# Moving the dense pieces among the steps of layer 1's attention

## The chip, the cores and the metric

The kernel runs on one core of one Trainium2 chip. Its time is the device time in microseconds; lower is better. Before the change three runs took 3043.94, 3046.15 and 3050.73 us, with a median of 3046.15 us.

## The reference

Two transformer layers run over `x` of 8 batches x 1024 tokens x 256. Layer 0 is windowed attention and a mixture of eight experts with a shared one. Layer 1, which the change touches, is block-sparse attention with 16 heads of 16 and blocks of 64 tokens, then a linear layer with ternary weights. Both layers normalize first and add their result to `x`.

```python
x = x + _L1_attn_ref(_layernorm(x, axis=-1), Wq, bq, Wk, bk, Wv, bv)
x = x + _L1_ffn_ref(_layernorm(x, axis=-1), weight, alpha, bias)
# in the attention: block 0 and block 15 of queries see all keys; block 1 and block 14
# see four blocks of keys; a block in the middle sees three neighbours, block 0 and block 15
```

The softmax subtracts each row's maximum, so scores are needed once for the maxima and again for the weights.

## The kernel before

**Two passes of scores.** `attention` (L377) serves both layers. A *round* of scores (`scores`, L392, matmuls at L404) makes the scores of one tile of 128 queries against the keys it meets, for four heads, in four PSUM tiles; VectorE takes the negated maximum of each (`maximum`, L414: L427, or L431 and L435 for the tile that sees all 1024 keys in two rounds). `into_q` (L439) transposes four tiles of maxima on TensorE (L442) and writes them into the queries (L446). Then `weights` (L448) makes the scores the other way round, with the maxima already subtracted (L459), in four PSUM tiles; ScalarE takes the exponential (L466), and GpSimd sets blocks that aren't met to zero (L1354). Two steps later `sums` (L477) multiplies them by v (L489), and `turned` (L501) transposes the result of half a batch (L504), which VectorE divides by the sum (L596, L597) and GpSimd adds to `x` (L1366).

**Steps.** One trip of the loop at L569 is a *step*. In layer 1 a batch has 4 groups of heads with 7 packs of weights and 9 rounds of scores, so 28 steps and 36 rounds: in every 7 steps, two have two rounds. In a batch these are steps 2, 6, 9, 13, 16, 20, 23 and 27. A step issues, in this order: weights (L459), the products of the step two back (L489), a round of scores (L404), what is due (transpositions L442 or L504), and, where there is a second round, the pieces due by the step's middle (`fill_until(step + 0.5)`) and that round; then the pieces due by its end (`fill_until(step + 1)`).

```python
                if some:
                    scores(*some.pop(0))
                for due, f in [x for x in later if x[0] <= step]:
                    later.remove((due, f))
                    f()
                if some:
                    fill_until(step + 0.5)
                    scores(*some.pop(0))
                fill_until(step + 1)
                step += 1
```

**Pieces.** What else a layer has to do is cut into pieces with due times in steps of the batch, written out by hand in `layer1` (L1400 to L1460). The order of issue is fixed by these times: all is recorded under a manual schedule, and each engine runs its instructions in that order. The pieces that use TensorE ("dense" ones: all 128 rows and columns) are, by line:

- L282, queries and keys (`qk_pieces`): 8 pieces for the second half of heads of batch b, in its own steps, and 8 for the first half of the next batch; ScalarE copies each out (L302, L314).
- L338, values (`v_pieces`): 8 pieces for the next batch; VectorE copies each out (L342).
- L235, transpositions of normalized rows (`norm_pieces`): piece `step(jp)` transposes pair jp-1, which ScalarE copies out (L248), and then has VectorE normalize pair jp (two instructions L223, one for each tile of the pair, into a buffer `xn` of which there are two).
- L1324, the ternary linear layer of the batch before (`product`): 8 pieces; VectorE adds each to `x` (L1330). Before it GpSimd adds the bias (L1319, `biased`).

Others use VectorE and GpSimd: statistics (L206 to L211), gathers of the experts' rows (an indirect DMA on GpSimd's queue, L1283) and their addition (L1291).

**PSUM.** Seven buffers of 128x512 (`ps_t`, L76) serve every tile but that of the products with v, in turn: a tile is written when the tile seven before it has been read.

Of the kernel before, what the change touches and what calls it, by code (L numbers as in the profile page):

```python
# [50 lines left out]
def seq_kernel(  # L51
# [135 lines left out]
    def piece(weight, f, *args, first=(), then=None):  # L187
        return weight, lambda: f(*args), first, then
# [1040 lines left out]
    def layer1():  # L1229
# [47 lines left out]
        def gathers(b):  # L1277

            w, ys = routed[b][2], {}

            def gather(j, n):
                y = ys[j, n] = pool.tile([128, D], F32, tag="y", name="y", bufs=16)
                nc.gpsimd.indirect_dma_start(  # L1283
                    out=y, out_offset=None, in_=made[:, :],
                    in_offset=bass.IndirectOffsetOnAxis(ap=place[b][:, n, j : j + 1], axis=0),
                )

            def add(j):
                xj = x_of[b][:, j, :]
                for n in range(2):  # L1290
                    nc.vector.scalar_tensor_tensor(  # L1291
                        xj, ys.pop((j, n)), w[:, j, n : n + 1], xj, ALU.mult, ALU.add
                    )

            return [
                piece(0.2, gather, j, n, first=[("placed", b)])
                for j in range(NT) for n in range(2)
            ], [piece(1.1, add, j, then=("added", b, j)) for j in range(NT)]

        def before_it(b):  # L1300
            qk_of[b], xnT_of[b] = {}, []
            norm = norm_pieces(
                b, "xnT2", xnT_of[b], "xnT", key_order=True,
                first=lambda jp: [("added", b, 2 * jp + 1)],
            )
            first = qk_pieces(b, 0, 1, wq_sb, wk_sb, xnT_of[b], qk_of[b])
            return gathers(b), norm, first, v_pieces(b, 1, wv_sb, xnT_of[b])
# [4 lines left out]
        def after_it(b):  # L1312

            xnT = []
            dst = out[b].rearrange("(t p) d -> p t d", p=128)

            def biased(jp):
                xp = x_of[b][:, pairs[jp], :]
                nc.gpsimd.tensor_tensor(xp, xp, bt, ALU.add)  # L1319

            def product(j):
                ps = psum_t()[:, 0:D]
                for kc in range(2):
                    nc.tensor.matmul(  # L1324
                        ps, lhsT=xnT[0][:, kc, j * 128 : (j + 1) * 128], rhs=wt_sb[:, kc, :],
                        start=(kc == 0), stop=(kc == 1),
                    )
                t = tile_at[j]
                xj = x_of[b][:, t, :]
                nc.vector.tensor_tensor(xj, ps, xj, ALU.add)  # L1330
                if j >= NT - 2:
                    nc.sync.dma_start(dst[:, t : t + 1, :], x_of[b][:, t : t + 1, :])
                elif j % 2:
                    nc.sync.dma_start(dst[:, t - 1 : t + 1, :], x_of[b][:, t - 1 : t + 1, :])

            norm = norm_pieces(
                b, "xnT", xnT, "normed", first=lambda jp: [("attended", b, 3, jp // 2)],
                tiles=tile_at, apart=b == B - 1,
            )
            return norm, [  # L1340
                piece(1.0, biased, jp, first=[("normed", b, jp)], then=("biased", b, jp))
                for jp in range(4)
            ], [piece(0.9, product, j, first=[("biased", b, j // 2)]) for j in range(NT)]
# [54 lines left out]
        def combining(gathered, x, at, adds, b):  # L1398

            gather, add = gathered  # L1400
            return [(0, [x], [piece(0.0, load, b)]), (0, at, gather), (0, adds, add)]

        beside = []
        for b in range(B + 1):
            lists = []
            if b == 0:
                (gather, add), (stats, scaled), first, values = before_it(0)

                rest = [piece(x[0], x[1]) for x in left_over]

                def some(n):
                    return [rest.pop(0) for _ in range(n)]

                begun = gather[:]
                for j, n in enumerate((3, 2, 1, 2, 1, 2, 1, 1)):
                    begun += some(n) + add[j : j + 1] + (stats[j // 2 : j // 2 + 1] if j % 2 else [])
                for x in scaled:
                    begun += [x] + (some(1) if len(rest) > 1 else [])
                lists.append((-1, -1e-6, begun + first + rest))
                lists.append((-0.95, -0.1, values))  # L1420
            if b < B:
                lists.append((
                    0, [0.4, 1.4, 2.2, 3.3, 4.4, 5.4, 6.2, 7.6],
                    qk_pieces(b, 1, 1, wq_sb, wk_sb, xnT_of[b], qk_of[b]),
                ))
            if b == B:
                (stats, scaled), biases, products = after_it(b - 1)
                scaled, turned = scaled[:4], scaled[4:]
                lists.append((
                    0, [-1.9, -0.9, -0.8, -0.7, 0.9, 0.92, 0.94, 0.96, 1.8, 1.9] + [2.5] * 14,  # L1430
                    stats[:2] + scaled[:2] + turned[:1] + biases[:1] + turned[1:2] + biases[1:2]
                    + products[:4] + stats[2:] + scaled[2:] + turned[2:] + biases[2:] + products[4:],
                ))
            elif b > 0:
                (stats, scaled), biases, products = after_it(b - 1)
                lists.append((0, [1.6, 2.8, 4.6, 5.5], stats))
                lists.append((0, [5.7, 7.4, 8.4, 10.3, 11.3], scaled))
                lists.append((0, [7.9, 8.8, 10.9, 11.8], biases))
                lists.append((0, [9.7, 10.5, 11.4, 12.6, 13.2, 13.8, 14.6, 15.6], products))
            if b + 1 < B:  # L1440
                gathered, (stats, scaled), first, values = before_it(b + 1)
                if b == 0:
                    lists.extend(combining(
                        gathered, 1.5, [0.5 + 0.4 * i for i in range(16)],
                        [3.5, 4.5, 5.5, 6.8, 7.5, 8.5, 9.5, 10.3], b + 1,
                    ))

                lists.append((0, [5.6, 7.6, 10.4, 10.7] if b == 0 else [-7.1, -3.6, 0.6, 10.6], stats))
                lists.append((0, [11.5, 12.4, 14.4, 15.4, 16.4], scaled))
                lists.append((0, [16.8, 17.3, 17.7, 18.4, 19.4, 20.2, 20.7, 21.3], first))  # L1450
                lists.append((0, [19.8, 21.7, 22.3, 23.2, 24.2, 25.3, 26.3, 27.2], values))
            if b + 2 < B:
                lists.extend(combining(
                    gathers(b + 2), 16.2, [12 + 0.6 * i for i in range(16)],
                    [18.6, 19.6, 21.4, 22.5, 24.7, 25.5, 26.5, 28.3], b + 2,
                ))
            if b + 3 < B:
                lists.append((0, [3.9], [piece(0.0, placed, b + 3)]))
            beside.append(lists)
# [10 lines left out]
    with ExitStack() as ctx1:  # L1470
        layer1()
# [76 lines left out]
```

## Time and profile before

| | |
|---|---|
| time of three runs | 3043.94, 3046.15, 3050.73 us |
| the profiled execution | 3047.95 us, of which its span 3046.2 us |
| mean granted TensorE clock | 0.991 |
| layer 1's attention in the trace | from about 1875 us to the end |
| one batch of it, 28 steps | 145.9 to 146.3 us (batches 2 to 4) |
| TensorE busy in such a batch | 144.2 to 144.7 us |
| VectorE, ScalarE, GpSimd busy in it | 105.8, 85.4, 53.4 us |

In the table of engines, PE is TensorE's matmuls and PEld its weight loads, DVE is VectorE, ACT ScalarE, POOL GpSimd. A line of the order in time has the start in us, the length of the group in us, the engine, the line of code, the operation, what it writes and reads, the engine's tile for PE (rows*columns of the array), the shapes, the count, and in brackets the engine's idle time before it and what ended that. A line of busy times by window has the window, its length, the busy time of PE, PEld, DVE, ACT and POOL with the number of instructions, the granted clock, the DMAs' share and GB/s. fp32 matmuls show as two instructions each.

### The profile page before, as it was taken

The numbers are of one execution on the slowest core, as the hardware profiler recorded it, in microseconds if no ns is written. First come the engines' busy times: TensorE is split into PE (matmuls) and PEld (weight loads), VectorE is DVE, ScalarE is ACT, GpSimd is POOL, SyncE is SP. The second block draws the span as 40 slices with busy tenths as digits, with TensorE's granted clock in tenths as the row PEclk, the third lists the DMA queues.
The fourth block names the chain that finished last, engine by engine and source line by source line (L and its number), as shares of the span: only waits on it lengthen the run. The fifth ranks groups of instructions, "written<-read, shape, count | busy, mean of one in ns | idle before, by whom it ended". The sixth has DMA issues, their size and how long they took to land. (4 is left out here: it accounts for less than half of the span.)

```text
span 3046.2 us, 81036 instructions
## 1 busy us (share of the span) xinstructions
PE 2967.0 (97%) x32684; PEld 1907.1 (63%) x32684; DVE 1896.5 (62%) x5996; ACT 1389.0 (46%) x2845; POOL 994.3 (33%) x2406
## 2 busy tenths in 40 slices
PE   8999999999999998999999998999999999999998
PEld 4455555555555545788888885555555555555554
DVE  5667676666667665344333345776767686767564
ACT  4454454444444442122222213555556555656554
POOL 4334454545453546000000011424242434243223
PEclk9999999999999999999999998999999999999998
DMA  3000101010101001666666642101010101010000
GB/s 107 2 2 16 42 17 41 19 39 19 40 22 36 24 26 46 217 208 213 230 211 213 213 147 62 35 9 52 7 57 2 57 2 57 6 54 6 12 13 19
DMA packets 109447, 198.18 MB, mean 65 GB/s; under 512 B 11152, under 2 KB 81296, under 8 KB 109072
## 3 DMA queue, kind: packets, MB, share of 16 engines
q1 hardware_dynamic: 96784, 159.43, 15.7%
q0 software_dynamic: 12288, 33.57, 3.5%
q8 instruction: 257, 4.21, 0.6%
q14 instruction: 118, 0.97, 0.1%
HBM read 139.22 MB, written 53.74 MB: 63 GB/s over the span
## 5 line engine op out<-in xcount | busy, mean ns | idle before, releaser
L466 ACT ACTIVATE w<-pst 128x512 f32<-128x512 f32 (+1 forms) x1664 | 834.7, 589 | 581.6 <-PE pst L459 560.4
L915 POOL TENSOR_SCALAR_AFFINE_SELECT w<-w 128x256 f32<-128x256 f32 x896 | 335.4, 406 | 525.1 <-ACT w L466 523.8
L427 DVE TENSOR_REDUCE maxima<-pst 128x1 f32<-128x320 f32 (+1 forms) x896 | 368.2, 473 | 215.2 <-PE pst L404 175.9
L422 DVE CUSTOM_DVE_ANT_0 junk<-pst,mask_mid 128x320 f32<-128x320 f32 x768 | 330.6, 486 | 181.1 <-PE pst L404 177.3
L489 PE MATMUL pso<-w,v 128*32 128x256 f32 (+5 forms) x6400 | 434.7, 388 | 2.1 <-ACT oT L498 2.1
L617 ACT ACTIVATE th<-pst 128x256 f32<-128x256 f32 (+1 forms) x309 | 117.0, 379 | 654.2 <-PE pst L611 622.6
L611 PE MATMUL pst<-xsT,of 128*128 128x256 f32 (+1 forms) x1704 | 383.6, 375 | 0.8 <-ACT xsT L1186 0.7
L611 PEld LDWEIGHTS pst<-xsT,of 128*128 128x128 f32 x1704 | 313.1, 191 | 40.4 <-ACT xsT L1186 0.9
L1354 POOL MEMSET w<- 64x128 f32 x768 | 151.8, 199 | 557.6 <-ACT w L466 531.5
L1283 POOL DMA_INDIRECT y<-made,from x128 | 122.2, 955 | 620.0 <-DVE h L622 587.4
L622 DVE SCALAR_TENSOR_TENSOR h<-th,pst 128x256 f32<-128x256 f32 (+1 forms) x309 | 128.2, 415 | 289.1 <-ACT th L617 281.5
L489 PEld LDWEIGHTS pso<-w,v 128*32 128x32 f32 x6400 | 157.9, 109 | 216.4 <-issue 154.8
L431 DVE TENSOR_REDUCE two<-pst 128x1 f32<-128x512 f32 x256 | 159.0, 684 | 114.1 <-PE pst L404 84.2
L631 PE MATMUL pst<-of,h 128*128 128x256 f32 x828 | 190.5, 379 | 0.0
L631 PEld LDWEIGHTS pst<-of,h 128*128 128x128 f32 x828 | 157.0, 190 | 21.2
L623 DVE TENSOR_TENSOR h<-h,pst 128x256 f32<-128x256 f32 (+1 forms) x309 | 128.3, 415 | 10.6
L211 POOL TENSOR_TENSOR rstd<-var,neg_half 128x4 f32<-128x4 f32 x64 | 67.3, 1052 | 186.8 <-DVE var L210 132.4
L1366 POOL TENSOR_TENSOR x<-x,ao 64x64 f32<-64x64 f32 (+1 forms) x192 | 78.6, 416 | 104.1 <-DVE ao L597 86.2
L206 DVE BATCH_NORM_STATS2 stats<-x 128x6 f32<-128x256 f32 x256 | 103.9, 406 | 1.2 <-POOL x L1366 0.9
L631 PE MATMUL pst<-shared_down,h 128*128 128x256 f32 x384 | 94.4, 395 | 8.6 <-issue 4.9
L1194 DVE COPY ys<-pst 128x512 f32<-128x512 f32 (+1 forms) x71 | 48.0, 676 | 84.6 <-PE pst L631 84.5
L422 DVE CUSTOM_DVE_ANT_0 junk<-pst,mask_last 128x256 f32<-128x256 f32 x128 | 46.7, 421 | 72.9 <-PE pst L404 72.9
(831 smaller groups left out, 4886.0 us busy)
## 6 DMA issues: line engine op xcount, KB each, us to landing
of<-in_w_up_dram SPq DMA_DIRECT2D x71, 768.0 KB, 4.9
of<-in_w_down_dram SPq DMA_DIRECT2D x71, 384.0 KB
xs<-bucket SPq DMA_DIRECT2D x67, 256.0 KB, 6.2
made<-ys SPq DMA_DIRECT2D x67, 256.0 KB, 2.1
x<-in_x_dram SPq DMA_DIRECT2D x32, 256.0 KB, 3.9
between<-x SPq DMA_DIRECT2D x8, 1024.0 KB
x<-between SPq DMA_DIRECT2D x32, 256.0 KB, 3.9
out_dram<-x SPq DMA_DIRECT2D x24, 256.0 KB, 3.1
```

The costliest lines, as they stand in the source:

```text
L422: nc.vector.tensor_tensor_reduce(out=junk[:, 0:many], in0=ps[:, 0:many], in1=mask, scale=-1.0, scalar=3e38, op0=ALU.add, op1=ALU.min, accu ...
L427: nc.vector.tensor_reduce(to[:, r, :], ps[:, 0:many], AX.X, ALU.max, negate=True)
L431: nc.vector.tensor_reduce(twos[0][:, r, n : n + 1], ps[:, 0:many], AX.X, ALU.max, negate=True)
L466: nc.scalar.activation(w[:, r, 0:n], ps[r][:, 0:n], AF.Exp)
L489: nc.tensor.matmul(columns(po[rows[r], :], to - 512 * half, many, step), lhsT=v_of[b % 2][:, kt, head : head + 32], rhs=w[:, r, n : n + many],
L611: nc.tensor.matmul(ps[:, part * GT : part * GT + n], lhsT=up_sb[:, kc, f0 : f0 + 128], rhs=xT[:, kc, :], start=(kc == 0), stop=(kc == 1),)
L622: nc.vector.scalar_tensor_tensor(h, th, 1.0, g, ALU.add, ALU.mult)
L623: nc.vector.tensor_tensor(h, h, u, ALU.mult)
L631: nc.tensor.matmul(ps[:, t * D : (t + 1) * D], lhsT=hs[fc][:, t * 128 : (t + 1) * 128], rhs=down_sb[:, fc, :], start=(fc == 0), stop=(fc = ...
L915: nc.gpsimd.affine_select(out=part, in_=part, compare_op=ALU.is_ge, fill=0.0, base=0, pattern=[[0, 2], [sign, 128]], channel_multiplier=-sign,
L1283: nc.gpsimd.indirect_dma_start(out=y, out_offset=None, in_=made[:, :], in_offset=bass.IndirectOffsetOnAxis(ap=place[b][:, n, j : j + 1], a ...
L1354: nc.gpsimd.memset(part, 0.0)
```

## The change

Only due times in `layer1` change; no instruction is added, removed or altered.

```diff
@@ -1420,7 +1420,7 @@
                 lists.append((-0.95, -0.1, values))
             if b < B:
                 lists.append((
-                    0, [0.4, 1.4, 2.2, 3.3, 4.4, 5.4, 6.2, 7.6],
+                    0, [0.4, 2.2, 2.8, 3.4, 4.4, 5.4, 6.2, 6.8],
                     qk_pieces(b, 1, 1, wq_sb, wk_sb, xnT_of[b], qk_of[b]),
                 ))
             if b == B:
@@ -1434,9 +1434,9 @@
             elif b > 0:
                 (stats, scaled), biases, products = after_it(b - 1)
                 lists.append((0, [1.6, 2.8, 4.6, 5.5], stats))
-                lists.append((0, [5.7, 7.4, 8.4, 10.3, 11.3], scaled))
-                lists.append((0, [7.9, 8.8, 10.9, 11.8], biases))
-                lists.append((0, [9.7, 10.5, 11.4, 12.6, 13.2, 13.8, 14.6, 15.6], products))
+                lists.append((0, [5.7, 7.4, 7.9, 10.3, 11.3], scaled))
+                lists.append((0, [7.6, 8.4, 10.9, 11.8], biases))
+                lists.append((0, [9.3, 9.8, 10.6, 12.6, 13.2, 13.8, 14.6, 15.6], products))
             if b + 1 < B:
                 gathered, (stats, scaled), first, values = before_it(b + 1)
                 if b == 0:
@@ -1447,8 +1447,8 @@
 
                 lists.append((0, [5.6, 7.6, 10.4, 10.7] if b == 0 else [-7.1, -3.6, 0.6, 10.6], stats))
                 lists.append((0, [11.5, 12.4, 14.4, 15.4, 16.4], scaled))
-                lists.append((0, [16.8, 17.3, 17.7, 18.4, 19.4, 20.2, 20.7, 21.3], first))
-                lists.append((0, [19.8, 21.7, 22.3, 23.2, 24.2, 25.3, 26.3, 27.2], values))
+                lists.append((0, [16.8, 17.3, 17.8, 18.4, 19.4, 20.2, 20.8, 21.4], first))
+                lists.append((0, [22.4, 23.2, 23.8, 24.6, 26.6, 27.2, 27.8, 29.4], values))
             if b + 2 < B:
                 lists.extend(combining(
                     gathers(b + 2), 16.2, [12 + 0.6 * i for i in range(16)],
```

What stands where then, in TensorE's order of a batch in the middle (scores are those of L404; "behind" is behind the second round, ahead of the next step's weights):

| step | before | after |
|---|---|---|
| 1 | L442, L282 | L442, L338 (the last values for this batch, which stood in step 27 or before) |
| 2 | L504, L282, scores | L504, L282, scores, L282 behind |
| 6 | L282, scores | L282, scores, L282 behind |
| 7 | L235, L282 | L235, L235 |
| 8 | L442, L235 | L442 |
| 9 | L504, scores, L1324 | L504, L1324, scores, L1324 |
| 11 | L442, L235, L1324 | L442, L235 |
| 19 | L504, L282, L338 | L504, L282 |
| 21 | L282, L338 | L282 |
| 23 | L504, L338, scores | L504, L338, scores, L338 behind |
| 25 | L442, L338 | L442 |
| 27 | L338, scores | L338, scores, L338 behind |

The other steps keep their pieces. In step 7 VectorE's two pairs of normalizations (L223) then follow each other, behind the maxima of step 7's scores (L431, L435). Batch 0 has neither L235 in steps 7 and 8 nor L1324 (they belong to the batch before); batch 7 has no values and no gathers for a next one. The table is the order in which the instructions are issued, not a time.

## The prediction

> **What bounds the kernel now.** I read the page first, then busy times for whole batches of layer 1, then the order in time around the pieces that move. The page:
>
> ```profile
> span 3046.2 us, 81036 instructions
> PE 2967.0 (97%) x32684; PEld 1907.1 (63%) x32684; DVE 1896.5 (62%) x5996; ACT 1389.0 (46%) x2845; POOL 994.3 (33%) x2406
> ```
>
> One batch of layer 1 (28 steps; batches counted from 0, this one is 3), the same columns, by window:
>
> ```profile
> 2315.82:2462.15 146.33, 144.72 (x2214) 85.22 (x2209) 105.77 (x265) 85.44 (x174) 53.41 (x144) 1.00 0.10 31
> ```
>
> TensorE is the bound and the clock is full, but its 99% hides waits: a matmul that waits for a PSUM buffer lies among others that run. The same block takes 1.09 us in one step and 2.30 in another (eight 512-wide matmuls of the weights, L459). The difference is a wait: seven PSUM buffers go round, so a tile needs the reader of the tile seven before it. Steps 2 and 3 of batch 2:
>
> ```profile
> 2184.47 0.80 PE L404 MATMUL pst<-k__24709,q__24707 32*64 32x128 f32 x32
> 2185.20 1.83 PE L459 MATMUL pst<-q__24706,k__24708 32*128 32x512 f32 x8
> 2185.37 1.67 DVE L427 TENSOR_REDUCE maxima<-pst 128x1 f32<-128x320 f32 x4
> 2186.96 0.32 PE L489 MATMUL pso<-w,v 128*32 128x128 f32 x4
> ```
>
> The second scores (L404), the weights (L459), VectorE's four maxima (L427), the products with v (L489). The fourth tile of weights needs the first maximum, done 0.48 us after 2185.37; L489 starts 1.11 us after that. This is the model for every term: a dense piece (0.96 to 1.06 us) ahead of such a wait costs only one more eviction (0.40 us, 0.33 for the 256-wide ones), since it makes the fourth tile need the second maximum; taking one away there gains as little.
>
> **The change, part by part** (steps of batch 2, from its order in time; every piece keeps its instructions, and adds no DMA).
>
> *Steps 2, 6, 23 and 27: a piece behind the second scores.* By the model: step 2, +0.40 (L489 after the second maximum, 2186.25 + 1.11, in place of 2186.96); step 6, second maximum at 2204.81, L489 at 2205.92 for 2205.58, +0.34; step 23, +0.40; step 27, +0.33. ScalarE's two copies of a query or key piece (2 x 0.56) come ahead of the exponentials, but the exponentials are next needed over 1 us later. VectorE's 0.41 for a v piece falls in gaps of over 1.7 us.
>
> *Step 1: a piece of v for one of queries or keys.* Same matmuls, 0. The products of step 2 wait for the part of v they read, not for this piece.
>
> *Step 9: one L1324 product between transposition and second scores.* Now the transposition takes 0.59 and the scores 1.20 (0.47 of it waiting for maxima). Then 0.49 + 0.96 + 0.73: the scores end 0.40 later. VectorE takes the product's addition (0.42) before the next maxima, so those and the weights behind them are 0.40 later too: +0.40 in all. *Step 11 loses it*: -0.87, but the next weights then wait for the third maximum (2228.02 + 1.11 = 2229.12 for 2229.58): -0.46.
>
> *Steps 19, 21, 25: a piece of v less.* Step 25: the weights' fourth tile needs the second maximum, not the third: -0.40. Step 21: -0.86, then steps 22 and 23 become like steps 1 and 2, which have the same pieces and wait 0.38 longer: -0.48. Step 19 saves 0.86 with nothing behind it, but step 20 has this:
>
> ```profile
> 2276.17 1.11 PE L404 MATMUL pst<-k__25578,q__25576 32*64 32x512 f32 x16
> 2276.68 0.95 POOL L1283 DMA_INDIRECT y<-made,from  x1 [0.30 <-ACT w L466]
> 2277.21 1.13 PE L282 MATMUL pst<-xnT__26517,wk_sb 128*128 128x256 f32 x4
> 2278.32 2.48 DVE L431 TENSOR_REDUCE two<-pst 128x1 f32<-128x512 f32 x4 [2.45 <-PE pst L282]
> ```
>
> The scores end at 2277.28, but VectorE starts on them at 2278.32, 0.69 after a gather's issue ended; where no gather runs (steps 6 and 27) it starts at once. In the changed kernel the scores end 0.86 earlier, at the end of the gather before (2276.37). If the hold spans both gathers, VectorE starts at the same moment and the gain is 0; if not, the gain is up to 1.5. I take -0.40 with gathers (batches 0 to 5), between 0 and the plain 0.86, and -0.84 in batch 6.
>
> *Steps 7 and 8: the second transposition of normalized rows (L235) comes to step 7, straight behind the first, and the keys piece that stood there goes to step 6.* This decides. The order in time before:
>
> ```profile
> 2207.63 0.66 PE L235 MATMUL pst<-ident,xn 128*128 128x128 f32 x4
> 2207.76 2.48 DVE L431 TENSOR_REDUCE two<-pst 128x1 f32<-128x512 f32 x4 [2.29 <-PE pst L404]
> 2208.12 1.03 PE L282 MATMUL pst<-xnT__24350,wk_sb 128*128 128x256 f32 x4
> 2209.08 1.16 PE L459 MATMUL pst<-q__24707,k__24709 32*128 32x128 f32 x24
> 2210.28 0.17 DVE L435 TENSOR_REDUCE maxima<-two 128x4 f32<-128x8 f32 x1
> 2210.36 0.73 DVE L223 TENSOR_SCALAR xn<-x,mv,rstd 128x256 f32<-128x256 f32 x2
> 2211.17 0.80 PE L404 MATMUL pst<-k__25577,q__25575 32*64 32x128 f32 x32
> 2212.39 0.60 PE L235 MATMUL pst<-ident,xn 128*128 128x128 f32 x4
> ```
>
> The second transposition reads what L223 writes at 2210.36 to 2211.09. L223 is queued on VectorE behind four maxima of 512 columns (L431, 2.48 us) and L435, and these begin only with the scores of step 7. Before, TensorE came to it at 2212.39, over a microsecond after. In the changed kernel it comes at 2208.12 (in this scale) and stands: two transposes can go when the first half is there (2210.76), two with the second (2211.09). Behind them on TensorE, in order, are all weights, products and scores of step 8; VectorE and ScalarE wait for those. Worked out: last transposes 2211.15, weights 2211.41; + 1.09 + 1.00 + 0.73 gives the transposition of the maxima at 2214.23 (its next 0.49 to 0.59 us lie beside the maxima); second maximum 2214.23 + 0.13 + 0.89 = 2215.25; L489 of step 9 at 2216.36, for 2214.43 before: **+1.93**. That is with the saved piece counted. Were nothing to wait, L489 would come at 2213.60: -0.83. The batches 1 to 7 have this pair, batch 0 not.
>
> *The sum without the clock.* A full batch (1 to 5): 0.40 + 0.34 + 1.93 + 0.40 - 0.46 - 0.40 - 0.48 + 0.40 - 0.40 + 0.33 = +2.06. Five: 10.3. Batch 6, without gathers: 1.6. Batch 7, steps 1 to 11 alone: 2.6. Batch 0 has no pair; two pieces leave its steps 1 and 7 without replacement (estimate -0.4 and -0.6, one or two evictions of 0.4 to 0.7 less); -0.8. In all **+13.7 us**.
>
> *The clock.* The stall leaves TensorE idle from 2208.29 to about 2210.82, 2.5 us, seven times. Windows at the layers' borders, TensorE's busy time first, then the granted clock:
>
> ```profile
> 1194.52:1197.93 3.41, 1.06 (x6) 0.61 (x5) 2.82 (x15) 0.00 (x0) 0.30 (x2) 1.00 0.00 0
> 1197.93:1201.35 3.42, 3.00 (x7) 2.46 (x8) 1.12 (x3) 0.00 (x0) 1.25 (x2) 0.50 0.11 38
> 1839.60:1843.00 3.40, 1.42 (x8) 1.23 (x9) 3.26 (x12) 0.66 (x3) 1.55 (x2) 1.00 0.00 0
> ```
>
> A window of 3.41 us in which TensorE worked 1.06 or 1.42 us is followed by one at half clock. The Trainium skill ("TensorE: Matmul & The Clock Gate", section "Why this matters for your kernels") says to avoid idle gaps over some 3 us; by that rule a gap of 2.5 us costs nothing and the sum stays 13.7. The rows say otherwise: the gap before 1197.93 was 2.8 us and the one before 1843.0 only 2.4. The page's section "What's actually happening" has the window free-running at 3413 ns, which these rows fit. If half a window's idleness is enough, a gap of 2.5 us fills half of one window in about three positions out of four: 5 of 7 batches, each 3.41 us at half clock, 1.7 us lost in a stretch of back-to-back TensorE work: 8.4 us. I take the rows; the ends are 0 and 7 x 1.7 = 12. **Sum +22.1**: the profiled execution, 3047.95 (span 3046.2 and 1.75 around it), becomes 3070; on the median of the runs, 3046.15, **3068**.
>
> **The rivals.**
> *A: the stall, the clock stays full.* For it: the skill's rule, and no half clock from 1884 to 2996 in spite of waits. Against it: the rows above, and those waits have matmuls between them. 3046.15 + 13.7 = 3060.
> *B: no stall (the other side).* VectorE would have to reach L223 before TensorE is through with the first transposition. Then each of seven batches is 2.76 better: 13.7 - 19.3 = -5.6, 3040.5. It turns at a wait of about 0.8 us per pair; the wait worked out is 2.5. Against it: four reductions of 0.68 us cannot begin before the scores end, and L223 stays behind them in VectorE's order.
> *C: nothing moves.* The pieces are the same in number and TensorE is busy 97%, so the order only changes who waits: 3046. Against it: the waits are of different kinds, some for one eviction, one for a whole queue.
> *D: worse.* Half clock for two windows at a time (1829.4 and 3020.6 show 6.8 us), and more waiting in step 20: 22 + 12 gives 3080.
>
> **How the numbers follow.** Stall with clock 0.55, A 0.25, B 0.07, C 0.07, D 0.06. Changes under 0.2% (6 us) can hardly be told from none. The likeliest is 3068, by itself 3061 to 3077. With A, whose low end has the step-20 gain in full (6 x 1.1 less: 3053), and part of D, the range is 3053 to 3079. Slower: likeliest, A, D and a little of C: 0.87; same 0.09 (C, and B's own figure is inside 0.2%); faster 0.04, B with step 20's gain.
>
> **What would show it.** In the order in time of the changed kernel, in each of batches 1 to 7, an L235 group with TensorE idle some 2.5 us ahead of it and released by L223; "PE L235 <- DVE xn L223" near 7 x 2.5 us in the waits, where it is absent between 1874 and 2996 us now; half clock for 3.4 us after some of these. Steps 2 to 3 and 6 to 7 longer by 0.3 to 0.4 us. The prediction is wrong if L235 is not idle there, or if steps 19 to 23 gain over 3 us a batch.

## The result and the profile after

The changed kernel takes **3061.68 us** (median of 4 runs, 3057.22 to 3062.91), the kernel before 3045.05 us (4 runs beside it, 3043.26 to 3050.73): ratio **1.0042 [1.0025, 1.0060]**, slower, by 12.8 us if the ratio is taken and by 16.6 if the medians are. The profiled execution of the changed kernel took 3057.22 us, its span is 3055.5; that of before took 3047.95 with a span of 3046.2.

Page of the changed kernel, span and engines:

```profile
span 3055.5 us, 81036 instructions
PE 2960.0 (97%) x32684; PEld 1898.0 (62%) x32684; DVE 1895.3 (62%) x5996; ACT 1388.4 (45%) x2845; POOL 997.9 (33%) x2406
```

Busy times of the changed kernel in batch 3 (window, length, busy time of PE, PEld, DVE, ACT, POOL, granted clock, DMA share, GB/s), from the same instruction to the same instruction as the row shown of before:

```profile
2316.66:2465.59 148.93, 145.29 (x2209) 84.68 (x2208) 105.61 (x265) 85.38 (x174) 53.57 (x144) 0.98 0.10 31
```

148.93 us in place of 146.33, a clock of 0.98 in place of 1.00, and TensorE now is idle for 3.6 us of it, where it was for 1.6. The order in time of the changed kernel, steps 7 and 8 of batch 2, shows where:

```profile
2206.70 0.65 PE L235 MATMUL pst<-ident,xn 128*128 128x128 f32 x4
2206.83 2.49 DVE L431 TENSOR_REDUCE two<-pst 128x1 f32<-128x512 f32 x4 [2.62 <-PE pst L404]
...
2209.35 0.16 DVE L435 TENSOR_REDUCE maxima<-two 128x4 f32<-128x8 f32 x1
2209.43 1.38 DVE L223 TENSOR_SCALAR xn<-x,mv,rstd 128x256 f32<-128x256 f32 x4
...
2209.98 0.74 PE L235 MATMUL pst<-ident,xn 128*128 128x128 f32 x4 [2.62 <-DVE xn L223]
...
2210.66 2.09 PE L459 MATMUL pst<-q__24707,k__24709 32*128 32x128 f32 x24
...
2212.68 1.63 PE L489 MATMUL pso<-w,v 128*32 128x384 f32 x16
```

The second L235 stands 2.62 us for L223, which sits on VectorE behind L431 and L435. The windows around it (same columns as above):

```profile
2206.98:2210.40 3.42, 0.80 (x8) 0.53 (x6) 3.38 (x9) 0.59 (x1) 0.00 (x0) 1.00 0.00 0
2210.40:2213.90 3.50, 3.50 (x34) 2.06 (x37) 0.40 (x2) 1.66 (x4) 0.00 (x0) 0.51 0.00 0
```

A window in which TensorE worked 0.80 of 3.42 us is followed by one at half clock: the weights of step 8 (L459) take 2.09 us, which before took 1.16, and the products (L489) 1.63. The waits of TensorE between 1874 and 3000 us have a row that the kernel before has not (us in total, times, longest):

```profile
PE pst L235 <- DVE xn L223: 18.3, 7, 2.6
```

Half clock follows after 6 of the 7 stalls, in batches 1, 2, 3, 4, 5 and 7; in batch 3 it lasts 6.8 us, in the others 3.4. Two more profiled executions of the changed kernel have the same row, 18.3 us in 7 times, and half clock after 5 and 6 of the 7. Taken along the borders at which the granted clock changes, 3.41 us apart, the three traces agree: 17 of the 21 stalls left a window with 0.79 to 1.52 us of TensorE work, and half clock followed each of these; the other four left 1.60 us or more in every window, and the clock stayed full.

**Where the time went, step by step.** A step's time is taken from its first weights (L459) to those of the next step. After minus before, in us, for batch 4 (with gathers) and batch 6 (without); like batches of a trace agree to some 0.05 in each step, but for the half clock in steps 7 and 8 and for steps 14, 17 and 18, in which gathers are issued and which differ by up to 0.5. Steps 4, 5 and 13 to 18, left out, add up to less than 0.1 in these two:

| steps | batch 4 | batch 6 |
|---|---|---|
| 0 (behind step 27 of the batch before) | -0.73 | -0.73 |
| 1, 2, 3 | +0.01 +1.06 -0.66 | 0.00 +1.06 -0.66 |
| 6, 7, 8 | +1.06 +1.70 +1.18 (half clock) | +1.04 +1.70 -0.44 (full clock) |
| 9, 10, 11, 12 | +0.44 -0.07 -0.87 +0.42 | +0.43 -0.07 -0.86 +0.42 |
| 19, 20, 21, 22 | -0.87 -0.84 -1.76 +0.06 | -0.86 0.00 -0.86 +0.06 |
| 23, 24 | +1.06 -0.66 | +1.06 -0.66 |
| 25, 26 | -0.67 +0.30 | -0.87 +0.47 |
| 27 | +1.66 | +1.06 |
| sum | +1.84 | +1.29 |

The eight batches together, up to the start of the last step, give +11.5 us in this trace. Without half clock a full batch gives only -0.2 to +0.4: the gain of steps 19 to 22 pays for the wait of steps 7 and 8. What is left of the loss is the clock, batches 6 and 7, and little else.

### The profile page after: what moved, and what is told of

It is laid out like the page before. It is cut to its first block, busy times and chain, and to the rows that moved or that the text cites. A ratio compares the mean times of both kernels' runs of the same rounds, so it can differ in the third digit from the quotient of the medians.

```text
span 3055.5 us, 81036 instructions
## 1 busy us (share of the span) xinstructions
PE 2960.0 (97%) x32684; PEld 1898.0 (62%) x32684; DVE 1895.3 (62%) x5996; ACT 1388.4 (45%) x2845; POOL 997.9 (33%) x2406
## 3 DMA queue, kind: packets, MB, share of 16 engines
q1 hardware_dynamic: 96784, 159.43, 15.5%
## 5 line engine op out<-in xcount | busy, mean ns | idle before, releaser
L489 PE MATMUL pso<-w,v 128*32 128x256 f32 (+5 forms) x6400 | 437.6, 390 | 2.0 <-ACT oT L498 2.0
L1283 POOL DMA_INDIRECT y<-made,from x128 | 122.7, 959 | 620.1 <-DVE h L622 587.5
L489 PEld LDWEIGHTS pso<-w,v 128*32 128x32 f32 x6400 | 158.5, 110 | 218.9 <-issue 149.6
L431 DVE TENSOR_REDUCE two<-pst 128x1 f32<-128x512 f32 x256 | 159.0, 684 | 109.3 <-PE pst L404 94.0
L623 DVE TENSOR_TENSOR h<-h,pst 128x256 f32<-128x256 f32 (+1 forms) x309 | 128.3, 415 | 10.6
L235 PE MATMUL pst<-ident,xn 128*128 128x128 f32 x384 | 64.4, 293 | 44.0 <-DVE xn L223 43.9
```

Of the source, the lines that this page charges most:

```text
L431: nc.vector.tensor_reduce(twos[0][:, r, n : n + 1], ps[:, 0:many], AX.X, ALU.max, negate=True)
L489: nc.tensor.matmul(columns(po[rows[r], :], to - 512 * half, many, step), lhsT=v_of[b % 2][:, kt, head : head + 32], rhs=w[:, r, n : n + many],
L623: nc.vector.tensor_tensor(h, h, u, ALU.mult)
```

## The experiments

Four sessions, each on another chip and with its own runs of the kernel before: the first for e0 to e3, the second for e4 to e6, the third for e7 to e10, the fourth for e11. Ratios are to the kernel before in the same session. The kernel before took 3048.49 us in the first and 3050.17 in the third, but 2991.25 and 2990.15 in the second and fourth; what lies behind that turned out to matter.

### First session: the pair, the wait, the clock

**e0, the changed kernel again**, as the bar for the three below.

> The changed kernel once more, on the same chip as the three others, for its intervals and for a second trace. Theory: the stall of step 7 is again 2.5 us in each of 7 batches, while the number of batches with half clock after it may differ (5 to 7), each 1.5 us: 3057 to 3063.

Measured: 3061.6 us, 1.0041 [1.0027, 1.0054]. As expected.

**e1, the pair undone.** The second transposition and normalization go back to step 8, and GpSimd's additions of the bias (L1319) to their old times; everything else stays changed. To the changed kernel:

```diff
-                lists.append((0, [5.7, 7.4, 7.9, 10.3, 11.3], scaled))
-                lists.append((0, [7.6, 8.4, 10.9, 11.8], biases))
+                lists.append((0, [5.7, 7.4, 8.4, 10.3, 11.3], scaled))
+                lists.append((0, [7.9, 8.8, 10.9, 11.8], biases))
```

> The changed kernel with its second transposition back in step 8 (times of the scaled and bias lists as before). Theory (the pair in step 7 stands 2.5 us behind VectorE's queue, and the clock falls to half after it): the 7 x 2.0 us of the stall and the some 10 us of half clock go, and what is left are the gains of steps 19 to 25: about 3035 to 3037 us, 0.3% under the kernel before; no wait of L235 for L223 in layer 1, no half clock between 1884 and 2996 us. Rival (the longer time comes from the pieces put behind the second scores): 3058 or more, since these all stay.

Measured: **3037.23 us, 0.9959 [0.9945, 0.9973]**, 24.4 less than e0. L235 no longer waits for L223 anywhere in the batches of layer 1, and no half clock lies between 1910 and 3015 us. Its second transposition in batch 2, and steps 7 and 8 there as a window:

```profile
2216.40 0.66 PE L442 MATMUL pst<-ident,maxima 128*128 128x128 f32 x4
2216.90 0.60 PE L235 MATMUL pst<-ident,xn 128*128 128x128 f32 x4
```

```profile
2208.98:2217.43 8.45, 8.45 (x134) 4.99 (x133) 4.99 (x13) 6.21 (x12) 1.38 (x7) 1.00 0.01 2
```

So the pair alone turns a gain of 11 us into a loss of 13: this part decides the sign.

**e2, the wait filled.** The pair stays as changed, but TensorE gets something to do in the wait: three matmuls whose result nobody reads (five lines added, and one argument altered elsewhere so that they run in these seven places alone; L235, L431 and L459 of the changed kernel are L240, L436 and L464 here, the added matmuls L234).

```diff
+            if apart is None and jp == 1:
+                for n in (512, 512, 256):
+                    nc.tensor.matmul(
+                        ps[:, 0:n], lhsT=ident, rhs=shared_up[:, 0, 0:n], start=True, stop=True
+                    )
```

> The changed kernel with three matmuls that lead nowhere (128x512, 128x512, 128x256, into the PSUM tile that the second transposition then overwrites) ahead of the second transposition in step 7, some 2.2 us of TensorE work in a wait of 2.5 us. Theory (idleness alone lowers the clock): the transposition still goes at the same moment, step 7 keeps its length, but the clock stays full and steps 8 are 3.4 us long: 10 us less than the changed kernel, about 3051. Rival A (the clock costs nothing beside the wait): 3061, as the changed kernel, or more if the added matmuls stick out.

Measured: **3051.95 us, 1.0009 [1.0000, 1.0018]**, 9.7 less than e0. Order in time, steps 7 and 8 of batch 2:

```profile
2210.64 2.31 PE L234 MATMUL pst<-shared_up,ident 128*128 128x512 f32 x6
...
2213.33 0.76 PE L240 MATMUL pst<-ident,xn 128*128 128x128 f32 x4 [0.38 <-DVE xn L223]
...
2214.02 1.16 PE L464 MATMUL pst<-q__24710,k__24712 32*128 32x128 f32 x24
```

Its window there, and its row of TensorE's waits:

```profile
2210.60:2214.00 3.40, 3.02 (x12) 1.40 (x10) 3.37 (x9) 0.58 (x1) 0.00 (x0) 1.00 0.00 0
```

```profile
PE pst L240 <- DVE xn L223: 2.6, 7, 0.4
```

L240 still goes at the same point behind L223, so the order costs what it cost; but TensorE works 3.02 of 3.40 us, the clock stays at 1.00 from 1888 us to the last step of batch 7, and the weights take 1.16 us again. The 9.7 us are the price of the half clock, separated from that of the wait. The same split comes out of the steps: at full clock the pair's steps 7 to 9 stand at +1.69 (batch 6), in e1 at -0.47, so the wait itself is 2.16 x 7 = 15.1 us, and 24.4 - 15.1 = 9.3 is left for the clock.

**e3, a piece of keys back between the two transpositions.** It makes the wait shorter without making the second L235 go any earlier:

```diff
-                    0, [0.4, 2.2, 2.8, 3.4, 4.4, 5.4, 6.2, 6.8],
+                    0, [0.4, 2.2, 2.8, 3.4, 4.4, 5.4, 6.2, 7.6],
```

> The changed kernel with the last keys piece due at 7.6 in place of 6.8, so that it stands between the two transpositions of step 7. Theory: the second transposition goes at the same moment after the scores, the wait shrinks to some 1.5 us, less than half of a window of 3.41 us, so the clock stays full; step 6 is 1.06 us shorter and the weights of step 7 wait 0.73 us more: per batch -0.3, and -10 us of half clock: 3049 (3047 to 3053). If a wait of 1.5 us were enough for the half clock: 3059.

Measured: 3054.26 us, 1.0018 [1.0009, 1.0027], 5 us above what was expected. Its row of waits, and two windows of its batch 3:

```profile
PE pst L235 <- DVE xn L223: 12.3, 7, 1.8
```

```profile
2355.48:2358.90 3.42, 1.67 (x20) 1.04 (x22) 3.22 (x8) 1.74 (x4) 0.00 (x0) 1.00 0.00 0
2358.90:2362.30 3.40, 3.40 (x44) 1.79 (x48) 0.00 (x0) 2.23 (x6) 0.66 (x4) 0.50 0.00 0
```

Steps 6 to 8 are 0.33 us a batch shorter than in the changed kernel at full clock, as the term for step 6 has it: in step 7 the piece lies wholly inside the wait. What was missed is the clock: waits of 1.75 us still brought half clock twice in seven (3.4 us each time, step 8 +1.56). In the window that did it TensorE had worked 1.67 us, just under half. But the same share did not always do it: five of the seven waits lay inside one window and left it 1.66 us of work, and in batches 2, 4 and 6 the clock stayed full. Batch 2:

```profile
2208.68:2212.10 3.42, 1.67 (x10) 1.19 (x10) 3.33 (x8) 1.61 (x3) 0.00 (x0) 1.00 0.00 0
2212.10:2215.51 3.41, 3.41 (x78) 2.23 (x77) 0.69 (x3) 2.38 (x5) 0.56 (x3) 1.00 0.00 0
```

So between 1.5 and 1.7 us of work the busy time alone does not tell what the clock will do.

### Second session: what the later pieces of v bring

**e4, the kernel before with the changed times of v alone.**

```diff
-                lists.append((0, [19.8, 21.7, 22.3, 23.2, 24.2, 25.3, 26.3, 27.2], values))
+                lists.append((0, [22.4, 23.2, 23.8, 24.6, 26.6, 27.2, 27.8, 29.4], values))
```

> The kernel before with the changed list of due times for values and nothing else. By the trace of the changed kernel: steps 19 to 22 -3.3 us a batch, 23 and 24 +0.4, 25 and 26 -0.4, 27 and 0 +0.9, and step 1 has one piece more than in the changed kernel, +0.8: -1.6 a batch with gathers, in all about -11 us, 3035. By the sizes of the prediction (steps 19 to 23 -0.9): +0.2 a batch, 3046.

**e6, the same, but with the last four times earlier**: the piece of step 25 stays where it was, none goes over into the next batch, and the one of step 26 comes ahead of the additions L1291 on VectorE:

```diff
-                lists.append((0, [19.8, 21.7, 22.3, 23.2, 24.2, 25.3, 26.3, 27.2], values))
+                lists.append((0, [22.4, 23.2, 23.8, 24.6, 25.3, 26.4, 27.2, 27.8], values))
```

> The kernel before with the values at 22.4, 23.2, 23.8, 24.6, 25.3, 26.4, 27.2, 27.8: as in the change, but the piece of step 25 stays (nothing goes to the next batch's first step), and that of step 26 comes ahead of the two additions due at 26.5. Theory: -3.3 in steps 19 to 22, +0.4 in 23 and 24, 0 in 25, and in step 27 the scores no longer wait 0.6 us for a v piece's copy that stands behind the additions: +0.3 in 27 and 0; -2.6 a batch with gathers, -0.9 in batch 6: 3029. If the 0.6 us in step 27 has another cause: 3033.

**e5, the kernel before with its gathers closer together** (each due 0.45 steps after the one before in place of 0.6), so that they are done ahead of step 20:

```diff
-                    gathers(b + 2), 16.2, [12 + 0.6 * i for i in range(16)],
+                    gathers(b + 2), 16.2, [12 + 0.45 * i for i in range(16)],
```

> The kernel before with the 16 gathers of a batch at 12 + 0.45 i in place of 12 + 0.6 i, so that none is issued in steps 19 to 21. Theory (a gather's issue on GpSimd's queue delays the signal that matmuls of that time are done): the scores of step 20 end 0.8 us and the weights of step 21 0.9 us sooner, so up to 10 us in six batches, less what the denser gathers of steps 13 to 18 cost more: 3037 (3034 to 3044). Rival (VectorE is late in step 20 since it has the copy of a v piece and two additions to do): no change in steps 20 and 21, 3045.

Measured: e4 2989.83 us, 0.9992 [0.9983, 1.0001]; e5 2990.78, 1.0001 [0.9992, 1.0010]; e6 **2986.36, 0.9983 [0.9973, 0.9993]**. In the second session the kernel before itself took 2991 us. The traces of the three show why in part: a full batch of layer 1 (2 or 3, with what the edits themselves move taken off) is 5.5 to 5.8 us shorter than in the profile before, all of it in steps 13, 14, 17, 18, 20 and 21, in which gathers (L1283) are issued, 0.7 to 1.2 us each. With nothing lost to the gathers, e5 has nothing to move and tells nothing of the theory; but its steps can stand for those of the kernel before, which has no trace here. Against them e4 gains nothing in step 20 and 0.86 in step 21, in all +0.02 a batch, and e6 -0.87. So e4 and e6 show what the later v pieces bring *without* that effect, and that the two differ by 0.9 a batch: in e4 step 27 costs 0.6 more and the last piece, now in steps 1 and 2, 0.7, and steps 25 and 26 take 0.4 less.

This is the order in time of the changed kernel around step 27 of batch 2:

```profile
2310.76 1.36 DVE L1291 SCALAR_TENSOR_TENSOR x<-y,w,x 128x256 f32<-128x256 f32 x2
...
2311.87 1.74 PE L404 MATMUL pst<-k__26875,q__26873 32*64 32x512 f32 x16
2312.04 0.41 DVE L342 TENSOR_TENSOR v<-pst,rows_sb 128x256 f32<-128x256 f32 x1
...
2312.51 0.22 PEld L404 LDWEIGHTS pst<-k__26875,q__26873 32*64 32x64 f32 x12 [0.44 <-DVE v L342]
```

The v piece of step 26 is due at 26.6, the two additions at 26.5. Its copy L342 therefore comes behind L1291, at 2312.04, the second tile of scores of step 27 waits for the buffer that it frees, and the scores take 1.74 us for 1.11. In e6 the piece is due at 26.4, its copy comes first, and the scores take 1.11 us:

```profile
2270.92 0.41 DVE L342 TENSOR_TENSOR v<-pst,rows_sb 128x256 f32<-128x256 f32 x1
2271.25 1.44 DVE L1291 SCALAR_TENSOR_TENSOR x<-y,w,x 128x256 f32<-128x256 f32 x2
2272.03 1.11 PE L404 MATMUL pst<-k__26875,q__26873 32*64 32x512 f32 x16
```

Step 27 gives +1.06 in place of +1.66.

### Third session: with the gathers' effect again

Here the kernel before takes 3050 us and its batches have the length of the first session. **e7, the kernel before, and e8, the changed kernel**, are the bars.

> The kernel before itself, for a trace from the same chip as the three others: ratio 1. If the signals of matmuls are held back during gathers here, step 20's second scores take 2.0 us and step 21's weights 2.0 us; if not, 1.2 and 1.1.

> The changed kernel. Theory: its time is the stall (14 us) and the half clock (some 10 us), less what steps 19 to 25 gain. Where gathers hold signals back: +13 to +17 us on the kernel before, as measured. Where they don't, steps 20 and 21 of the kernel before have no wait to lose, and the change costs about 10 us more: +22 to +27 us. Rival (the gain in steps 19 to 21 is VectorE's, which has a copy of v less to do): the same +13 to +17 us in both cases.

Measured: e7 3050.79 us, 1.0005 [0.9997, 1.0014]; e8 3062.11, 1.0041 [1.0028, 1.0054]. In e7's trace the gathers hold: the second scores of step 20 take 2.1 us, the weights of step 21 2.13. e8 is 11.9 us above the kernel before, a little under the +13 to +17 that both the theory and its rival gave for this case, so it can't tell them apart; e10 does.

**e10, the times of e6 once more.**

> The kernel before with the values at 22.4, 23.2, 23.8, 24.6, 25.3, 26.4, 27.2, 27.8. Where gathers hold signals back: -2.6 us a batch, -15 us, ratio 0.995. Where they don't: -0.9 a batch, -5 us, ratio 0.998, as on the chip of the first try.

Measured: **3034.73 us, 0.9950 [0.9937, 0.9963]**, 15.4 less than before and faster than both kernels. The same source gained 4.9 us in the second session. By step, in batch 2, against e5 in the second session and e7 in the third:

| steps | e6, second session | e10, third session |
|---|---|---|
| 0 | -0.73 | -0.73 |
| 19 | -0.86 | -0.87 |
| 20 | 0.00 | -0.86 |
| 21 | -0.86 | -1.79 |
| 22, 23, 24 | +0.06 +1.06 -0.67 | +0.06 +1.06 -0.66 |
| 25, 26 | +0.20 -0.13 | +0.20 -0.13 |
| 27 | +1.06 | +1.06 |
| sum, 13 to 18 with it | -0.86 | -2.57 |

All the difference lies in steps 20 and 21, 1.8 us a batch. That answers the rival of e8: VectorE has the same copy less to do in both, and gains there in one only. (It was idle for 2.45 us ahead of step 20's scores in the row shown of before.) What the chip does there can be seen best in step 13, which the two share. Order in time of e10:

```profile
2237.72 1.11 PE L404 MATMUL pst<-k__25577,q__25575 32*64 32x512 f32 x16
2238.58 0.96 POOL L1283 DMA_INDIRECT y<-made,from  x1 [0.30 <-ACT w L466]
...
2240.17 1.29 DVE L431 TENSOR_REDUCE two<-pst 128x1 f32<-128x512 f32 x2 [2.58 <-PE pst L1324]
```

and of e6, the same instructions:

```profile
2201.25 1.11 PE L404 MATMUL pst<-k__25577,q__25575 32*64 32x512 f32 x16
2202.11 0.96 POOL L1283 DMA_INDIRECT y<-made,from  x1 [0.30 <-ACT w L466]
...
2202.42 1.89 DVE L431 TENSOR_REDUCE two<-pst 128x1 f32<-128x512 f32 x3 [1.32 <-PE pst L404]
```

In both the gather is issued 0.86 us after the scores began, and ends 1.82 after. In e6 VectorE starts on the scores 1.17 us after they began, as soon as they are through. In e10 it starts 2.45 us after, 0.63 behind the end of the gather's issue. It is the same program in the same order, and TensorE's next matmuls (L1324, at 2238.77 and 2202.30) begin 1.05 us after the scores in both. In one session VectorE gets at the finished scores while GpSimd issues a gather, in the other only behind it. That it is the signal of TensorE's end which is held, and not the end itself, is inferred: the ends of matmuls in these traces are modelled.

**e9, the gathers of e5 once more.**

> The kernel before with the gathers of a batch at 12 + 0.45 i. Where gathers hold signals back: steps 20 and 21 some 1.7 us a batch shorter, steps 13 to 18 up to 1 us longer: -5 to -10 us. Where they don't: no change, as on the chip of the first try.

Measured: **3088.18 us, 1.0124 [1.0109, 1.0139]**, 38 us slower: the wrong sign. Steps 20 and 21 do gain, 0.8 and 0.9 in each batch of 0 to 5, as the theory had it. But order in time, steps 17 and 18 of batch 2:

```profile
2284.91 0.94 POOL L1283 DMA_INDIRECT y<-made,from  x1 [0.30 <-issue]
...
2286.15 0.95 POOL L1283 DMA_INDIRECT y<-made,from  x1 [0.30 <-issue]
...
2287.41 0.95 POOL L1283 DMA_INDIRECT y<-made,from  x1 [0.30 <-issue]
2287.50 0.48 PE L459 MATMUL pst<-q__25575,k__25577 32*128 32x128 f32 x2
2289.64 1.68 DVE L427 TENSOR_REDUCE maxima<-pst 128x1 f32<-128x320 f32 x4 [7.93 <-remote]
...
2290.19 1.17 PE L459 MATMUL pst<-q__25575,k__25577 32*128 32x128 f32 x7 [2.20 <-DVE maxima L427]
```

Five gathers follow each other from 2282.38 to 2288.36, 0.3 us apart. The scores of step 17 (L404) began at 2283.02; VectorE starts on them at 2289.64. TensorE runs out of PSUM buffers and stands for 2.20 us, and half clock comes on top. Steps 17 to 19 lose 2.9 to 6.6 us a batch, and steps 13 and 14 another 1.4 to 2.1 in batches 1 to 5. So the hold is not 0.6 us for a gather: here it lasts as long as the row of gathers does.

### Fourth session: the gathers spread out

**e11, e6 with the gathers further apart**, over steps 1 to 17 in place of 12 to 21, in the batches after the first:

```diff
-                    gathers(b + 2), 16.2, [12 + 0.6 * i for i in range(16)],
+                    gathers(b + 2), 16.2, [12 + 0.6 * i if b == 0 else 1.2 + 1.05 * i for i in range(16)],
```

> The kernel of e6 (seven values pieces moved) with the gathers of batches 1 to 5 spread over the batch, at 1.2 + 1.05 i in place of 12 + 0.6 i, so that nearly every one stands alone on GpSimd's queue. Theory (what is held back lasts from the first gather of a row of them to half a microsecond after the last): one gather alone holds for some 1.5 us and a row of two or three for up to 3.5, so more of it is hidden: where gathers hold signals back some 2 to 3 us a batch less than e6 in steps 13 to 18, less what the earlier steps pay: 3020 to 3032 where e6 has 3035. Rival (each gather costs about the same wherever it stands): as e6, 3035. Where gathers don't hold signals back: as e6.

Measured: 2987.3 us, 0.9989 [0.9980, 0.9997]. The kernel before took 2990.15 beside it: the gathers held nothing here, so this says only that spreading them does no harm, not whether it helps where they do.

## Why the prediction was right, and what in it was not

It said 3068 us, 22 more than before, and slower; measured were 3061.7, 12.8 to 16.6 more. The mechanism named for the sign is shown: with the pair undone (e1) the rest gains 11 us, with the wait filled (e2) two fifths of the pair's loss goes. The size is another matter. Two terms of the sum were mis-sized, in opposite directions, the larger by some 15 us, as much as the whole measured loss; that the time still lies inside the range owes something to luck and to a range drawn wide enough for a clock that stays full. Per full batch (1 to 5), in us, measured without half clock:

| term | forecast | measured |
|---|---|---|
| steps 1 to 3 | +0.40 | +0.41 |
| step 6, weights of 7 | +0.34 | +0.33 |
| steps 7 to 9, the pair | +1.93 | +2.03 |
| steps 9 to 10 | +0.40 | +0.33 |
| steps 11 to 12 | -0.46 | -0.45 |
| steps 19 to 22 | -0.88 | **-3.4** |
| steps 23, 24 | +0.40 | +0.40 |
| steps 25, 26 | -0.40 | -0.37 |
| step 27, 0 | +0.33 | **+0.93** |
| sum | +2.06 | +0.2 |

**The pair.** The wait was put at 2.5 us, seven times; it was 2.62, and 18.3 in all. Rival B (no wait) was excluded for the reason given: L223 stays behind the four maxima. No run has the pair without its wait. e1, which takes the pair apart, gains 24.4 us, by its steps 15.1 for the wait, which leaves 9.3 for the clock; the text had 19.3 for rival B without any clock, and 8.4 for the clock.

**The model of the fourth tile.** A dense piece behind the second scores costs one eviction, not its own 1.06 us. Steps 1 to 3, 6, 9 to 12 and 23 to 26 came within 0.07 us of it. The step itself gets 1.06 longer and the next 0.66 or 0.73 shorter.

**The clock.** The trace's rows were taken over the rule of the Trainium skill ("TensorE: Matmul & The Clock Gate", "Why this matters for your kernels"), by which only gaps over some 3 us are to be avoided; the runs side with the rows. Gaps of 2.6 us brought half clock after 6, 5 and 6 of the 7 stalls in three traces, 5 being forecast, and e2 priced it at 9.7 us. In the first trace it makes 10.6 us for a forecast 8.4: a window costs about 1.5, and where two follow each other 2.8, which the working did not have (it stood in rival D). The free-running window of 3413 ns in the page's section "What's actually happening" fits the 3.4 and 6.8 us that are seen.

**Steps 19 to 22, the term that failed.** -0.88 was forecast, -3.4 measured. There are two parts. In step 20 the text weighed two cases, a gain of 0 if the hold spans both gathers and of up to 1.5 if not, and took -0.40 between them; the latter is what happens, and somewhat more: -1.7 in steps 19 and 20. Order in time of the changed kernel, step 20 of batch 2, answering the rows shown of before:

```profile
2277.82 1.11 PE L404 MATMUL pst<-k__25574,q__25572 32*64 32x512 f32 x16
2277.94 0.96 POOL L1283 DMA_INDIRECT y<-made,from  x1 [0.16 <-issue]
2278.87 1.13 PE L282 MATMUL pst<-xnT__26517,wk_sb 128*128 128x256 f32 x4
2279.00 2.48 DVE L431 TENSOR_REDUCE two<-pst 128x1 f32<-128x512 f32 x4 [0.93 <-PE pst L404]
```

The scores are through as the gather's issue ends (2278.90), and VectorE starts at 2279.00: 1.18 us after the scores began, where before it was 2.15. In step 21 the same effect, which the text did not reckon with there, brings another 0.9 of gain; batch 6, which has no gathers, and the second session, where they hold nothing, both have -0.86 in step 21 and 0 in step 20. The rest of the miss, 0.3 us, is in steps 21 to 22 of batch 6: -0.80 for the -0.48 that was read off steps 1 and 2.

The prediction named "steps 19 to 23 gain over 3 us a batch" as what would make it wrong. Steps 19 to 22 do gain 3.4; with the later piece in step 23 it is 2.3.

**Step 27, the other term.** +0.33 forecast, +0.93 measured, because VectorE's copy of the v piece comes behind two additions. The text said that VectorE's 0.41 us for a v piece "falls in gaps of over 1.7 us"; the order on VectorE, not its free time, decides here. Batch 6, which has no additions, gives +0.33.

**The sum.** Without the clock 13.7 us were forecast and about 2.5 come out: steps 19 to 22 over batches 0 to 6 bring some 15.5 more gain, step 27 in six batches takes 3.6 back, the small differences 0.7. With 10.6 for the clock that is 13.1, between the 12.8 of the ratio and the 16.6 of the medians. The two profiled executions differ by only 9.3, for reasons outside the change: that of before has a half clock of its own in step 21 of batch 7 (1.6 us) and a last step 1.0 longer, and layer 1 starts 1.2 later in it. The measured time is thus nearer to rival A's 3060 than to the 3068 of the likeliest case, though A's reason, a clock that stays full, is refuted: the clock's loss is there, and a gain elsewhere nearly the size of it.

**Still open.** Why gathers hold TensorE's signals in two sessions and not in the two others isn't known; as each session had its own chip, chip and time can't be told apart. The changed kernel was not run where they don't; by the steps it should lose about 1.75 us more there in each of six batches, the gain in steps 20 and 21 that e4 and e6 lack.

## What to carry to other kernels

Before a TensorE instruction is moved ahead, look at the engine that makes its operand and at what is queued in front of it there: the wait is counted from that queue's end, and where it left a window of 3.4 us with 1.5 us of work or less, the slowdown behind it came on top, 9.3 us on 15.1 here. A dense piece between scores and weights costs only what it delays the reader of the buffer needed next, so pieces can be moved for tenths of a microsecond where their own length is one; e10, which moves only the pieces of v and keeps each copy ahead of VectorE's longer additions, takes 0.5% off where gathers hold, and 0.17% where they don't (e6). Where a step is longer than its like in a batch without gathers, compare the two before pricing a move there.

## What was not expected of the hardware

- Where GpSimd issues indirect gathers (0.95 us each, 0.3 us apart), VectorE and ScalarE can start on scores and pieces that TensorE finished during an issue only some 0.6 to 1.5 us after the last issue of the row ends: VectorE 0.63 behind one gather (e10), and behind a row of five VectorE 1.28 us, 6.6 us after the start of the scores, and ScalarE (L314) 1.47 us (e9). Scores that end 0.03 us behind an issue are read at once (step 20 of the changed kernel). A batch with gathers is 5.5 us longer for it. In two of four sessions it did not happen at all, and the kernel before took 2991 us in place of 3049. Between the spans of its profile and of e5's lie 56.6 us: batches 1 to 5 make 27.6 of them, batch 0, in which the gathers of two batches are issued and which begins at half clock, 11.9, batch 7 2.1, and 14.9 lie ahead of layer 1's attention, unexplained.
- Half clock came after a stall of only 1.75 us, in two of the five windows in which TensorE so worked 1.66 of 3.41 us (e3); filling the longer stall with matmuls that nobody reads (2.31 us) was worth 9.7 us over seven of them. Busy time as a trace shows it isn't all of it: in the profile before, half clock also follows the window from 2993.33 to 2996.74 us, in which TensorE shows 3.00 us of work. A group of eight matmuls of the weights takes 2.77 us there, for 1.09 elsewhere, so waits may lie inside what shows as busy; the cause is open.
- Two half-clock windows in a row can follow one stall of 2.6 us that lies across a border. Windows of the changed kernel in batch 3:

```profile
2353.79:2357.20 3.41, 1.29 (x20) 0.42 (x4) 2.61 (x6) 1.21 (x3) 0.00 (x0) 1.00 0.00 0
2357.20:2360.61 3.41, 2.91 (x28) 2.36 (x28) 1.32 (x5) 0.59 (x1) 0.00 (x0) 0.50 0.00 0
2360.61:2364.02 3.41, 3.41 (x53) 1.47 (x50) 0.00 (x0) 2.54 (x5) 1.59 (x8) 0.50 0.02 5
2364.02:2367.43 3.41, 3.41 (x52) 1.94 (x60) 2.28 (x5) 1.63 (x4) 1.65 (x3) 1.00 0.00 0
```

Of batch 5:

```profile
2654.18:2657.59 3.41, 3.16 (x32) 2.49 (x36) 1.07 (x4) 0.59 (x1) 0.00 (x0) 0.50 0.00 0
2657.59:2661.00 3.41, 3.41 (x67) 2.22 (x68) 1.64 (x5) 2.54 (x5) 1.83 (x9) 1.00 0.00 0
```

The window of batch 3 with 1.29 us of work is followed by half clock, as expected. But so is the next, in which TensorE was busy 2.91 us at half clock with the last 0.5 us of the stall. In batch 5 a half-clock window with 3.16 us gave the full clock back. Behind the stalls in the three traces of the changed kernel, a second half-clock window followed each that had 2.69 to 2.97 us and none that had 3.16 or more; why is open.
